# Query and key stores of a transformer block: parts in tiles of their own, the subtraction on VectorE for half of the work, reads spread over steps

## The chip, the core and the metric

The kernel runs on one core of one Trainium2 chip. The metric is the device time in microseconds (us). The kernel before took 2427.64 us (median of three runs, 2426.45 to 2430.05). One more run was profiled; it took 2427.2 us, and all times below that are not called a median are from it.

## The reference

The program is one conditioned transformer block on `x` of 2 x 2048 x 512 in float32. The rows of the batch are called row 0 and row 1.

```python
mod = silu(condition) @ Wada + bada
sh_a, sc_a, gt_a, sh_m, sc_m, gt_m = split(mod, 6, axis=1)
xm = layernorm(x, g1, be1) * (1 + sc_a) + sh_a
x = x + gt_a * attention(xm, Wqkv, Wproj, bproj)      # 16 heads of 32, causal
xm = layernorm(x, g2, be2) * (1 + sc_m) + sh_m
h = gelu(xm @ W1 + b1)                                # 512 -> 2048
x = x + gt_m * (h @ W2 + b2)                          # 2048 -> 512
```

The change touches the stage that makes queries, keys and values (`xm @ Wqkv`), once for each row of the batch.

## The kernel before, in words

**Order of the stages.** Queries, keys and values of row 0 (0 to 241 us of the profile), attention of row 0 (to about 780 us), projection of row 0 with the start of row 1, queries, keys and values of row 1 (841 to 1060 us), attention of row 1, its projection, and the two feed-forward layers for all tokens.

**A group and a unit.** `Qkv.run` (lines 1017 to 1075) takes the 2048 tokens of a row in four groups of 512. A group has six units: four of `keys_and_queries`, one for each 128 channels, and two of `values`. A unit multiplies 2 x 2 blocks with seven products in place of eight (Strassen's scheme in the form of Winograd), so it has seven steps, each of two products of 128 x 128 by 256. After each step `tick` counts one; a group has 42 ticks. The last step of a unit (`direct`) is made after the first two steps of the next one. The first unit of row 0 is made in a plain way instead (`plain`). From the second group on, `tick` also issues score products of the attention to come, as many as a plan of costs says.

**High and low parts.** Queries and keys are stored as a rounded part (hi, type float32r) and the rest (lo). `split` (line 940) rounds a tile of 128 x 512 with ScalarE (line 943) and subtracts that from the value with GpSimd (line 944). Both parts lie in one tile `hl` of two halves; the low half also serves as the accumulator while the unit's products come in. ScalarE writes a first partial result into it (line 938), VectorE adds others (lines 950 and 956). There are four such tiles, so two units' worth, and a tile is free when its store has landed.

**Stores and reads back.** `stored` (line 905) writes a tile to DRAM in one transfer of 512 KB. After the keys of the first unit of a group, it issues eight reads of 256 KB from DRAM right away (lines 319 and 336): they spread the first four heads' keys and queries over the partitions as attention wants them, and they need the stores just issued to have landed. All these transfers are issued by SP, whose queue works in order.

**What else uses the queues.** In the same stages weights for the feed-forward layers are prepared by `Pieces` (line 1077): SP reads a piece (lines 1102, 1111), GpSimd makes four sums of it for the seven-product scheme (line 1123), and GpSimd's own queue stores it (lines 1139, 1143). The reads and sums go by tick numbers in `pieces.plan` (lines 1384 and 1440). A piece of the first layer is read as 4 x 128 KB and stored as 896 KB; a piece of the second as 8 x 128 KB, stored as 7 x 448 KB. `load_wada` (line 1249) reads 2 MB of modulation weights in ticks 7 and 56 of row 0.

**Who sets the order.** TensorE's products and the operations wrapped in `act` keep the order of the program text; the rest is placed by the scheduler of the tile layer when the program is built. Each engine then works through its list in order, so an instruction that waits holds up all that stands behind it on its engine.

Of the kernel before, what the change touches and what calls it, by code (L numbers as in the profile page):

```python
# [8 lines left out]
F32 = mybir.dt.float32  # L9
# [18 lines left out]
def dit_block_kernel(  # L28
# [264 lines left out]
    class Row:  # L293
# [18 lines left out]
        def load_keys(self, c, g, n=1):  # L312

            for q in range(g, g + n):
                tok = slice(q * MT, (q + 1) * MT)
                t = self.key_tile(c, q)
                self.kst[c, q] = t
                for r in range(4):
                    nc.sync.dma_start(
                        t[r * HD : (r + 1) * HD].bitcast(F32),  # L320
                        kd[self.b][c][r % 2, :, tok].rearrange("(h d) t -> d h t", d=HD),
                    )
# [9 lines left out]
        def load_queries(self, u):  # L332
            c, i = units[u]
            t = bp.tile([P, HC, QB], F32R, tag="qst", name="qst", bufs=AHEAD + 1)
            for r in range(4):
                nc.sync.dma_start(
                    t[r * HD : (r + 1) * HD].bitcast(F32),
                    qd[self.b][c][r // 2, :, i * QB : (i + 1) * QB].rearrange(
                        "(h d) t -> d h t", d=HD
                    ),  # L340
                )
            self.qst[u] = t
# [440 lines left out]
    class Qkv:  # L783
# [6 lines left out]
        def __init__(self, row, qp, psum):  # L790
            self.row, self.qp, self.psum = row, qp, psum
            self.xts, self.xmT, self.ops = {}, {}, {}
            self.w = qp.tile([P, 7, HK, D], F32, tag="wqk", name="wqk")
            self.t = {
                n: qp.tile([P, HK, HALF_T], F32, tag=f"t{n}", name=f"t{n}")
                for n in (S1, S2, A22)
            }
# [107 lines left out]
        def stored(self, g, f, which, hl):  # L905
# [4 lines left out]
            nc.sync.dma_start(  # L910
                dst[:, :, tok].rearrange("l p t -> p l t"), hl.bitcast(F32)
            )
            if f == 0 and which == 1:
                row.load_keys(0, g)
                row.load_queries(g)

        def keys_and_queries(self, g, f, hp):

            ops = self.operands(g)
            hls = [  # L920
                hp.tile([P, 2, MT], F32R, tag="hl", name="hl", bufs=4) for _ in range(2)
            ]

            def part(i, j):
                d = hls[i].bitcast(F32)
                return d[:, 1, j * HALF_T : (j + 1) * HALF_T]
# [13 lines left out]
            def split(i):  # L940
                hl = hls[i]
                d = hl[:, 1].bitcast(F32)
                nc.scalar.copy(hl[:, 0], d)  # L943
                nc.gpsimd.tensor_tensor(hl[:, 1], d, hl[:, 0].bitcast(F32), ALU.subtract)  # L944
                self.stored(g, f, i, hl)
# [18 lines left out]
        def plain(self, g, f, hp):  # L964
# [3 lines left out]
            for which in range(2):  # L968
                box = []
                for k in range(C):  # L970
                    def run(which=which, k=k, box=box):
# [7 lines left out]
                        if k < C - 1:  # L979
                            return  # L980
                        hl = hp.tile([P, 2, MT], F32R, tag="hl", name="hl", bufs=4)
                        scale = HD**-0.5 if which == 0 else 1.0
                        nc.scalar.activation(hl[:, 0, :], box[0], AF.Copy, scale=scale)
                        nc.vector.scalar_tensor_tensor(
                            hl[:, 1, :], box[0], scale, hl[:, 0, :].bitcast(F32),
                            ALU.mult, ALU.subtract,
                        )
                        self.stored(g, f, which, hl)
# [28 lines left out]
        def run(self, hp, also, early=()):  # L1017
# [3 lines left out]
            for g in range(NG):  # L1021
                at = [0]

                def tick():
# [15 lines left out]
                    if g > 0 and n == 2:  # L1040
                        self.token_sum(g, A22)
                    also(g, n)
# [31 lines left out]
            for step in late:  # L1074
                step()

# [155 lines left out]
    with pool("wada") as wp, pool("qkv0") as qp, pool("hl0") as hp, pool(  # L1232
# [138 lines left out]

        def room_k():
# [12 lines left out]
        for f, (room, load, start) in enumerate((  # L1385
            (room_v, 4, 12), (room_v, 25, 36), (room_v, 46, 54), (room_k, 56, 63),
            (room_q, 66, 73), (room_k, 80, 87), (room_q, 91, 98), (room_k, 105, 112),
# [9 lines left out]
    with pool("qkv1") as qp, pool("ps_qkv1", bufs=6, space=PSUM) as ps_mm:  # L1397
# [29 lines left out]
        with pool("hl1") as hp:  # L1427
# [12 lines left out]
            for f, (room, load, start) in enumerate((  # L1440
                (room_2, 0, 6), (room_1, 16, 24), (room_2, 39, 46),
# [549 lines left out]
```

## Time and profile before

| | us |
|---|---|
| median of three runs | 2427.64 |
| profiled run: its time | 2427.2 |
| profiled run: its span, first to last instruction | 2424.7 |
| TensorE busy in the span | 2326.1 (96%) |
| VectorE, ScalarE, GpSimd busy | 1404.1, 1009.9, 1147.5 |
| granted TensorE clock, mean | 0.985 |

TensorE's busy share is 96% over the whole span, but the page's row of forty slices shows it lower in the first two slices and in the fifteenth and sixteenth, which lie in the stages of queries, keys and values. "Busy" in such a row includes time at a lowered clock, so a row of the granted clock stands beside it. The share of the DMA engines is the mean over 16 engines of the time that packets took; in these rows it can go slightly over 1.

### The profile page before, as it was taken

The page shows a single profiled execution, that of the slowest core. Times are in us where ns is not written, and L with a number is a line of the kernel's source. Part 1 is how long each engine was busy: PE and PEld are TensorE (multiplying, and loading weights), DVE is VectorE, ACT ScalarE, POOL GpSimd, SP SyncE. Part 2 cuts the span into 40 slices and gives each one's busy share as a digit, 9 for nine tenths or more (in the row PEclk, how much of TensorE's full clock was granted, in tenths as well). Part 3 has the DMA queues.
Part 4 walks back from the last instruction along what each step waited for, and adds up shares of the span by engine and source line. Part 5 has one row for each costly group of instructions (what it writes and reads, how often), then busy time and mean ns, then how long its engine had stood idle before and what let it go on. Part 6 is the DMA issues. An engine that isn't in the chain of part 4 may idle for free.

```text
span 2424.7 us, 34152 instructions
## 1 busy us (share of the span) xinstructions
PE 2326.1 (96%) x12033; PEld 1413.6 (58%) x12033; DVE 1404.1 (58%) x2930; ACT 1009.9 (42%) x1952; POOL 1147.5 (47%) x1291
## 2 busy tenths in 40 slices
PE   5799999999999977999999999999999999999998
PEld 3687555555554466865555555444486487477467
DVE  3366766666665623676677667474274365366356
ACT  3343555555556133345555555532332332332321
POOL 7441798878884594239889787651000000000000
PEclk9899999999999988999999999999999999999999
DMA  8865323241132775461412313254253353444333
GB/s 288 298 201 164 72 58 79 62 97 40 49 135 79 256 262 175 135 165 40 102 40 75 74 32 113 93 181 165 76 174 131 121 169 122 148 145 141 135 121 126
DMA packets 159492, 311.61 MB, mean 129 GB/s; under 512 B 15520, under 2 KB 47820, under 8 KB 157528
## 3 DMA queue, kind: packets, MB, share of 16 engines
q1 hardware_dynamic: 154464, 285.52, 38.7%
q0 software_dynamic: 4480, 23.36, 2.4%
q8 instruction: 94, 1.54, 0.3%
q14 instruction: 78, 0.64, 0.1%
q10 hardware_dynamic: 376, 0.55, 0.1%
HBM read 229.95 MB, written 87.29 MB: 131 GB/s over the span
## 4 chain that ended last, share of the span: by engine, by line
PE 82%; DMA 5%; POOL 5%; issue 3%; DVE 2%; SPq 1%; ACT 1%; POOLq 0%; DVEq 0%; ACTq 0%
PE ps_a L204 20%; PE st L204 19%; PE o L204 11%; PE ps_b L204 10%; PE s L204 9%; PE ps_c L204 5%; PE sm L204 4%; PE ps_o L204 3%; DMA k<-hl 2%; DMA q<-hl 1%; POOL kst L1123 1%; POOL hl L944 1%; PE ps_xt L212 1%; POOL ee L621 1%; DVE mx L468 1%
## 5 line engine op out<-in xcount | busy, mean ns | idle before, releaser
L593 ACT ACTIVATE e<-st 128x512 f32<-128x512 f32 (+1 forms) x1152 | 573.8, 579 | 429.5 <-PE st L204 369.8
L621 POOL TENSOR_TENSOR ee<-ee,e 128x512 f32<-128x512 f32 x424 | 528.9, 1285 | 4.4 <-ACT e L593 4.2
L468 DVE TENSOR_REDUCE mx<-s 128x1 f32<-128x512 f32 x604 | 407.4, 687 | 198.7 <-PE s L204 197.5
L204 PE MATMUL s<-kst,qst 128*128 128x512 f32 (+3 forms) x1032 | 419.1, 410 | 6.8 <-DVE mx L468 6.3
L204 PE MATMUL st<-qst,kst 128*128 128x512 f32 (+3 forms) x1280 | 409.3, 387 | 0.0
L204 PE MATMUL ps_a<-sum,w 128*128 128x256 f32 (+1 forms) x1088 | 346.6, 454 | 0.0
L204 PE MATMUL o<-e,vv 128*32 128x512 f32 (+3 forms) x2560 | 300.6, 538 | 1.9 <-POOL e L599 1.9
L463 DVE CUSTOM_DVE_ANT_0 junk<-s,causal 128x512 bf16<-128x512 f32 (+3 forms) x428 | 208.7, 488 | 136.2 <-PE s L204 128.8
L204 PEld LDWEIGHTS st<-qst,kst 128*128 128x128 f32 x1280 | 227.5, 188 | 94.0 <-issue 61.9
L204 PEld LDWEIGHTS ps_a<-sum,w 128*128 128x128 f32 x1088 | 206.4, 190 | 109.7 <-issue 91.3
L204 PEld LDWEIGHTS s<-kst,qst 128*128 128x128 f32 x1032 | 195.3, 189 | 120.9 <-DVE mx L468 58.7
L621 POOL TENSOR_TENSOR ee<-e 128x512 f32<-128x512 f32 x168 | 210.5, 1286 | 103.0 <-ACT e L593 102.7
L944 POOL TENSOR_TENSOR hl<-hl 128x512 fp32r<-128x512 f32 x62 | 78.8, 1270 | 198.8 <-ACT hl L943 166.6
L599 POOL TENSOR_SCALAR_AFFINE_SELECT e<-e 128x128 f32<-128x128 f32 (+1 forms) x384 | 121.9, 350 | 99.3 <-ACT e L593 96.5
L204 PE MATMUL st<-fold,sel 32*128 32x512 f32 (+1 forms) x1152 | 148.6, 481 | 0.5
L204 PEld LDWEIGHTS st<-fold,sel 32*128 32x128 f32 x1152 | 59.2, 181 | 143.2 <-ACT e L593 86.8
L1570 DVE TENSOR_TENSOR h<-c,ps_b 128x512 f32<-128x512 f32 x32 | 22.0, 687 | 202.4 <-PE ps_b L204 202.4
L204 PEld LDWEIGHTS o<-e,vv 128*32 128x32 f32 x2560 | 61.4, 108 | 101.7 <-issue 78.8
L204 PE MATMUL ps_b<-sum,w 128*128 128x256 f32 (+1 forms) x384 | 120.6, 450 | 0.0
L1744 ACT ACTIVATE h<-h,cols 128x512 f32<-128x512 f32 x96 | 69.2, 722 | 118.6 <-DVE h L1570 118.6
L468 DVE TENSOR_REDUCE mx<-st 128x1 f32<-128x512 f32 x164 | 112.6, 687 | 4.1 <-PE st L204 1.3
L204 PE MATMUL ps_a<-t,wqk 128*128 128x256 f32 x248 | 67.2, 400 | 39.3 <-ACT hl L938 37.4
(204 smaller groups left out, 3095.4 us busy)
## 6 DMA issues: line engine op xcount, KB each, us to landing
qst<-q SPq DMA_DIRECT2D x128, 256.0 KB
kst<-k SPq DMA_DIRECT2D x128, 256.0 KB
w<-w1d SPq DMA_DIRECT2D x32, 896.0 KB
w<-w2d SPq DMA_DIRECT2D x28, 1024.0 KB
w<-w2d SPq DMA_DIRECT2D x28, 768.0 KB
q<-hl SPq DMA_DIRECT2D x32, 512.0 KB
k<-hl SPq DMA_DIRECT2D x32, 512.0 KB
o<-ot SPq DMA_DIRECT2D x32, 256.0 KB
```

Source lines behind the costliest of these rows:

```text
L204: return tc.keep_in_program_order(nc.tensor.matmul(*args, **kw))
L212: return tc.keep_in_program_order(nc.tensor.transpose(dst, src, ident[:n, :n]))
L463: nc.vector.tensor_tensor_reduce(junk[:, :w], s[:, :w], causal[:, QB - w :], 1.0, MASKED, ALU.add, ALU.max, m,)
L468: nc.vector.tensor_reduce(m, s[:, :w], axis=AX.X, op=ALU.max)
L593: act(nc.scalar.activation(e[:, :w], sts[h][:, :w], AF.Exp))
L599: nc.gpsimd.affine_select(d, d, pattern=[[0, len(tiles)], [1, P]], compare_op=ALU.is_ge, fill=0.0, base=0, channel_multiplier=-1,)
L621: act(engine.tensor_tensor(dst, x, y, ALU.add))
L944: nc.gpsimd.tensor_tensor(hl[:, 1], d, hl[:, 0].bitcast(F32), ALU.subtract)
L1123: nc.gpsimd.tensor_tensor(part(n), part(x), part(y), op)
L1570: act(nc.vector.tensor_tensor(dst, x, y, ALU.add))
L1744: nc.scalar.activation(d, ps, AF.Gelu, bias=col(r_b1 + half * HF + f, 1))
```

## The change

Six edits, all in the stage of queries, keys and values:

1. The tile `hl` of two halves becomes two tiles, `hi` and `lo`. There are three `hi` tiles, and five `lo` tiles for row 0, six for row 1.
2. `stored` issues two transfers of 256 KB, one for each part, in place of one of 512 KB.
3. The subtraction that makes the low part runs on VectorE for the first two groups of a row, and on GpSimd as before for the other two.
4. The eight reads back of keys and queries are kept in a list, and `tick` issues one of them in each tick from the tenth on.
5. In row 0 the pieces of the first feed-forward layer are read and summed later: the first is summed from tick 38 (before 12), the others are read from tick 58 on (before 25), and the last uses another part of the value tile as its room.
6. In row 1 the third piece of the second layer is read at tick 47 and summed from tick 56 (before 39 and 46).

```diff
@@ -312,14 +312,20 @@
         def load_keys(self, c, g, n=1):
 
             for q in range(g, g + n):
-                tok = slice(q * MT, (q + 1) * MT)
-                t = self.key_tile(c, q)
-                self.kst[c, q] = t
-                for r in range(4):
-                    nc.sync.dma_start(
-                        t[r * HD : (r + 1) * HD].bitcast(F32),
-                        kd[self.b][c][r % 2, :, tok].rearrange("(h d) t -> d h t", d=HD),
-                    )
+                for load in self.key_loads(c, q):
+                    load()
+
+        def key_loads(self, c, q):
+            tok = slice(q * MT, (q + 1) * MT)
+            t = self.kst[c, q] = self.key_tile(c, q)
+
+            def load(r):
+                nc.sync.dma_start(
+                    t[r * HD : (r + 1) * HD].bitcast(F32),
+                    kd[self.b][c][r % 2, :, tok].rearrange("(h d) t -> d h t", d=HD),
+                )
+
+            return [lambda r=r: load(r) for r in range(4)]
 
         def key_tile(self, c, q):
             tag = f"kst{c % 2}{q}"
@@ -330,16 +336,23 @@
             return self.key_tile(0, q).bitcast(F32).rearrange("p h t -> p (h t)")
 
         def load_queries(self, u):
+            for load in self.query_loads(u):
+                load()
+
+        def query_loads(self, u):
             c, i = units[u]
             t = bp.tile([P, HC, QB], F32R, tag="qst", name="qst", bufs=AHEAD + 1)
-            for r in range(4):
+            self.qst[u] = t
+
+            def load(r):
                 nc.sync.dma_start(
                     t[r * HD : (r + 1) * HD].bitcast(F32),
                     qd[self.b][c][r // 2, :, i * QB : (i + 1) * QB].rearrange(
                         "(h d) t -> d h t", d=HD
                     ),
                 )
-            self.qst[u] = t
+
+            return [lambda r=r: load(r) for r in range(4)]
 
         def load_sums(self, u0, u1):
 
@@ -789,7 +802,7 @@
 
         def __init__(self, row, qp, psum):
             self.row, self.qp, self.psum = row, qp, psum
-            self.xts, self.xmT, self.ops = {}, {}, {}
+            self.xts, self.xmT, self.loads = {}, {}, []
             self.w = qp.tile([P, 7, HK, D], F32, tag="wqk", name="wqk")
             self.t = {
                 n: qp.tile([P, HK, HALF_T], F32, tag=f"t{n}", name=f"t{n}")
@@ -907,23 +920,24 @@
             row, b = self.row, self.row.b
             tok = slice(g * MT, (g + 1) * MT)
             dst = (qd if which == 0 else kd)[b][f]
-            nc.sync.dma_start(
-                dst[:, :, tok].rearrange("l p t -> p l t"), hl.bitcast(F32)
-            )
+            for n in range(2):
+                nc.sync.dma_start(dst[n, :, tok], hl[n].bitcast(F32))
             if f == 0 and which == 1:
-                row.load_keys(0, g)
-                row.load_queries(g)
+                self.loads = row.key_loads(0, g) + row.query_loads(g)
+
+        def hi_tile(self, hp):
+            return hp.tile([P, MT], F32R, tag="hi", name="hi", bufs=3)
+
+        def lo_tile(self, hp):
+            return hp.tile([P, MT], F32R, tag="lo", name="lo", bufs=5 + self.row.b)
 
         def keys_and_queries(self, g, f, hp):
 
             ops = self.operands(g)
-            hls = [
-                hp.tile([P, 2, MT], F32R, tag="hl", name="hl", bufs=4) for _ in range(2)
-            ]
+            los = [self.lo_tile(hp) for _ in range(2)]
 
             def part(i, j):
-                d = hls[i].bitcast(F32)
-                return d[:, 1, j * HALF_T : (j + 1) * HALF_T]
+                return los[i].bitcast(F32)[:, j * HALF_T : (j + 1) * HALF_T]
 
             def product(ps, n, new):
                 for k in range(HK):
@@ -938,11 +952,12 @@
                 nc.scalar.activation(part(i, j), ps, AF.Copy, scale=scale)
 
             def split(i):
-                hl = hls[i]
-                d = hl[:, 1].bitcast(F32)
-                nc.scalar.copy(hl[:, 0], d)
-                nc.gpsimd.tensor_tensor(hl[:, 1], d, hl[:, 0].bitcast(F32), ALU.subtract)
-                self.stored(g, f, i, hl)
+                hi, lo = self.hi_tile(hp), los[i]
+                d = lo.bitcast(F32)
+                nc.scalar.copy(hi, d)
+                engine = nc.vector if g < 2 else nc.gpsimd
+                engine.tensor_tensor(lo, d, hi.bitcast(F32), ALU.subtract)
+                self.stored(g, f, i, (hi, lo))
 
             def last(ps, i, j):
                 d = part(i, j)
@@ -978,14 +993,13 @@
                         )
                         if k < C - 1:
                             return
-                        hl = hp.tile([P, 2, MT], F32R, tag="hl", name="hl", bufs=4)
+                        hi, lo = self.hi_tile(hp), self.lo_tile(hp)
                         scale = HD**-0.5 if which == 0 else 1.0
-                        nc.scalar.activation(hl[:, 0, :], box[0], AF.Copy, scale=scale)
+                        nc.scalar.activation(hi, box[0], AF.Copy, scale=scale)
                         nc.vector.scalar_tensor_tensor(
-                            hl[:, 1, :], box[0], scale, hl[:, 0, :].bitcast(F32),
-                            ALU.mult, ALU.subtract,
+                            lo, box[0], scale, hi.bitcast(F32), ALU.mult, ALU.subtract
                         )
-                        self.stored(g, f, which, hl)
+                        self.stored(g, f, which, (hi, lo))
                     steps.append(run)
             return steps
 
@@ -1039,6 +1053,8 @@
                         act(nc.scalar.activation(first, eps, AF.Exp))
                     if g > 0 and n == 2:
                         self.token_sum(g, A22)
+                    if n > 9 and self.loads:
+                        self.loads.pop(0)()
                     also(g, n)
                     if g > 0 and n >= 7:
 
@@ -1073,6 +1089,7 @@
                     late = steps[6:]
             for step in late:
                 step()
+            assert not self.loads
 
     class Pieces:
 
@@ -1369,6 +1386,9 @@
         def room_v():
             return [(0, blocks_of(value_rows(row, 4, 8), w1p)[:, :7])]
 
+        def room_w():
+            return [(0, blocks_of(value_rows(row, NT - MTT, NT), w1p)[:, :7])]
+
         def room_k():
             return [(0, blocks_of(spare_k[1], w1p)[:, :7])]
 
@@ -1383,8 +1403,8 @@
 
         pieces.plan(FC // 2, room_2, 5, 17)
         for f, (room, load, start) in enumerate((
-            (room_v, 4, 12), (room_v, 25, 36), (room_v, 46, 54), (room_k, 56, 63),
-            (room_q, 66, 73), (room_k, 80, 87), (room_q, 91, 98), (room_k, 105, 112),
+            (room_v, 4, 38), (room_k, 58, 68), (room_q, 62, 73), (room_k, 84, 93),
+            (room_q, 88, 98), (room_k, 108, 116), (room_q, 112, 121), (room_w, 101, 126),
         )):
             pieces.plan(f, room, load, start)
         qkv.run(hp, also, ((0, 0),))
@@ -1438,7 +1458,7 @@
                 ]
 
             for f, (room, load, start) in enumerate((
-                (room_2, 0, 6), (room_1, 16, 24), (room_2, 39, 46),
+                (room_2, 0, 6), (room_1, 16, 24), (room_2, 47, 56),
             ), FC // 2 + 1):
                 pieces.plan(f, room, load, start)
             qkv.run(hp, also)
```

## The prediction

> **What bounds the kernel now.** I read the page first, then eight windows cut where the first products of the groups of tokens start (four of row 0, four of row 1), then who waited for the stores, then the chain of waits at single places.
>
> The windows, with TensorE's (PE) busy time, its granted clock and the share of the DMA engines near the end of each line:
>
> ```profile
> core 0: us, PE busy (x) PEld busy (x) DVE busy (x) ACT busy (x) POOL busy (x), PEclk, DMA share, GB/s
> 26.48:82.58 56.10, 37.15 (x166) 30.31 (x164) 16.37 (x40) 22.48 (x47) 44.62 (x56) 0.88 0.94 313
> 82.58:141.25 58.67, 46.64 (x217) 38.71 (x216) 22.09 (x68) 20.38 (x45) 20.94 (x24) 0.85 0.72 237
> 141.25:192.63 51.38, 50.16 (x250) 41.32 (x249) 33.49 (x90) 17.54 (x40) 19.58 (x22) 1.00 0.57 187
> 192.63:241.00 48.37, 45.35 (x207) 37.12 (x206) 32.10 (x75) 14.98 (x33) 10.17 (x8) 1.00 0.64 177
> 840.79:906.99 66.20, 49.75 (x193) 40.70 (x192) 16.00 (x39) 20.84 (x47) 55.77 (x67) 0.85 0.77 255
> 906.99:966.75 59.76, 47.43 (x202) 40.43 (x200) 20.93 (x67) 20.27 (x45) 28.69 (x35) 0.83 0.56 188
> 966.75:1015.50 48.75, 47.30 (x226) 39.95 (x225) 32.45 (x85) 17.73 (x40) 10.15 (x8) 1.00 0.41 130
> 1015.50:1060.00 44.50, 42.89 (x196) 35.77 (x195) 30.62 (x69) 14.66 (x32) 10.16 (x8) 1.00 0.63 178
> ```
>
> The reader is to see two kinds of group. In the last two of each row TensorE idles 1.2 to 3.0 us; in the first two, which I call dense, 12.0 to 19.0 us, 59.8 us in sum, and its clock is lowered besides. In ten-us windows of these stretches, busy time times (1 - clock) sums to 19.7 us.
>
> What the engines waited for, from the view of the tile `hl`:
>
> ```profile
> L943 ACT CAST hl<-hl x62: 607/618/626, 34.6 to 1048.4; 128x512 fp32r<-128x512 f32 x62
> L944 POOL TENSOR_TENSOR hl<-hl x62: 1255/1270/1291, 38.0 to 1049.1; 128x512 fp32r<-128x512 f32 x62
> ...
>   DMA q<-hl: 27.2, 8
>   DMA k<-hl: 24.5, 9
> ```
>
> ScalarE could not start on a tile for 51.7 us because its last store had not landed; TensorE's gaps follow from that. The chain of waits shows how long a landing takes, alone and behind other transfers:
>
> ```profile
> 32.72 4.43 DMA k<-hl
> ...
> 931.89 11.90 DMA k<-hl
> ```
>
> And SP's timeline shows why the largest gap (15.27 us to 59.35) came about: eight reads back and eight 256 KB reads of modulation weights stand ahead of stores whose data had been ready for long.
>
> ```profile
> 38.95 1.38 SPq L336 DMA_DIRECT2D qst<-q  x3
> 40.38 10.30 SPq L1263 DMA_DIRECT2D vv<-in_L_cond_Wada_dram  x8
> 52.17 0.38 SPq L910 DMA_DIRECT2D q<-hl  x1
> ```
>
> The product order of TensorE is the same in the two programs as built, so the change can act only through such waits.
>
> **The tiles.** A step is two products, 0.87 us undisturbed (ps_b starts at 31.18, ps_c at 32.05). Before, a unit's key tile was that of the unit two back, free seven steps after its rounding: 7 x 0.87 = 6.1 us. In them must fit 0.62 (rounding) + 1.27 (subtraction) + 0.36 (issue, SP's rows of line 910) + 4.43 (landing) = 6.7 us. It does not fit even with no queue. After, with two thirds of a unit more, a `hi` tile is written again ten steps on, 8.7 us, for 0.62 + 0.36 + 4.43 = 5.4 us, and a key `lo` tile ten steps on for 6.1 us. So 2.6 to 3.3 us of queueing are free, where 0.6 was missing.
>
> **Reads and weight pieces.** A spread read comes a tick apart (about 1 us), so a store finds few of them ahead, not 2 MB. In row 0's first group the modulation weights are now issued before the reads back, when the queue holds 1.5 MB of pieces at most; the first stores then follow at about 39 us, not 52. Of row 0's pieces, three reads (0.5 MB each) and two stores (0.9 MB each) leave the dense groups: 3.4 MB, at 313 GB/s / 0.94 = 333 GB/s 10.2 us of all DMA engines. They go to groups three and four, whose share rises from 0.57 and 0.64 by 10.2 us in 99.8; hidden there behind TensorE, price 1 us, up to 7 if a burst meets the reads back. Row 1's third piece moves 8 to 10 ticks and stays in the same group: nothing, or 3 us either way.
>
> **What is late next is the DMA.** Shares times lengths: 52.7 + 42.2 + 51.0 + 33.5 = 179.4 us of work in the dense groups, 169.2 without the moved pieces, in 240.7 us. TensorE's floor there is 240.7 - 59.8 - 19.7 + 3.2 (two gaps of 1.9 and 1.3 us of another cause) = 164. So the DMA engines need as long as TensorE. How full can they be? The first group reaches 0.94; the first 100 us of the kernel 0.85. I take 0.90: 169.2 / 0.90 = 188, a gain of 53 us; at 0.94 61, at 0.85 42. With the floor alone it would be 76.
>
> **The subtraction on VectorE.** 30 subtractions leave GpSimd (30 x 1.27 = 38 us), whose dense groups in row 1 are full: 55.77 of 66.20 busy. VectorE gets 30 x 0.69 (line 877, same shape) = 21 us in some 190, at 40% load: room enough. But it is a wait in VectorE's in-order list: behind it stand the additions of lines 950 and 956 and the score maxima. A product into the bank read by 956 comes two steps later, so 1.74 us of delay are free. And the two engines get in each other's way:
>
> ```profile
> L877 DVE TENSOR_TENSOR t<-xmT,t x16: 650/692/6049, 22.4 to 1015.7; 128x512 f32<-128x512 f32 x16
> ...
> 820.20 1.25 POOL L1210 TENSOR_TENSOR xt<-xt,bgate 128x512 f32<-128x512 f32 x1
> ...
> 819.63 6.05 DVE L877 TENSOR_TENSOR t<-xmT,t 128x512 f32<-128x512 f32 x1
> ```
>
> Of 14 such VectorE operations beside GpSimd's work, 13 took 0.67 to 2.03 us and one 6.05, until GpSimd paused. A 6.05 costs TensorE 6.05 - 0.69 - 1.74 = 3.6 us; the others nothing. About 19 of the 30 will meet GpSimd at work (6 in the first group, 2 in the second, 8 and 3 in row 1). I take two long ones among the eight of row 1's first group, where GpSimd is unbroken, and one in fourteen of the other 11: 2.8 x 3.6 = 10, less 2 for GpSimd's relief in row 1's third gap, 8 us. Bounds: 0, and all 19 long, 69 us.
>
> The Trainium skill (SBUF — State Buffer, "SBUF: two separate sides") says that a VectorE operation with two SBUF inputs and a reading GpSimd operation exclude each other for a whole instruction, whoever starts first. By that a wait would end with one GpSimd operation, 1.27 us, inside the free 1.74, and the price would be 0, the sum 8 us lower; the row of 6.05 us says that it can be several.
>
> **Two stores for one.** 64 more issues x 0.36 = 23 us of SP, which waited 73.2 us for line 944 in row 0's stage alone. In full stretches some of it delays a store: 2 us; 0 to 6. [...] In the trace eight 256 KB reads were taken in 10.30 us, 1.3 us each against 4.43 for a landing alone, so they overlap.
>
> **Sum.** 53 - 8 - 2 - 1 = 42 us. 2427.2 - 42 = 2385; the median is 0.4 us above the profiled run, which does not matter here. About 0.2% (5 us) is what a measurement of this kernel can tell from no change.
>
> **Rivals.**
>
> *The DMA engines give back half.* For it: shares of 1.02 to 1.04 in 40 to 80 us and 100 to 120 us, where even stores issued first landed after 8 to 12 us, more than the 8.7 us a tile now has. Against it: those followed 2 MB bursts. If such landings stay, each of four units in four dense groups still loses 1 to 2 us, and row 0's gaps only shrink: gain 10 to 28, about 2407.
>
> *VectorE starves behind GpSimd: slower.* One mechanism, in row 1's first group and row 0's first, where GpSimd sums pieces without a pause. It decides from the point where a contended subtraction takes 0.69 + 1.74 + 50/19 = 5.1 us in the mean; at 6.05 for all 19 it costs 69 against 50 gained: about 2446. For it: the 6.05 row, with the same kind of GpSimd work. Against: 13 of 14.
>
> *It does not do what it says.* Three `hi` tiles are fewer than four `hl` tiles; if rounding waits for them as long as the first write did, the 51.7 us stand under another name, time within 5 us of before. Against: ten steps for 5.4 us.
>
> **How the numbers follow.** Forecast (gain 29 to 70) 0.61; DMA half 0.19; starved, slower 0.15; nothing 0.05. Faster 0.80, same 0.05, slower 0.15. The range runs from 2358 (0.94 full, no price for VectorE, and some of the 7.3 us of idle time in the light groups) to 2424, which leaves out the starved case and a part of the even one. The forecast's own range is 2358 to 2398.
>
> **What the profile after would show.** Right: the four dense groups at 43, 50, 52 and 52 us or less, no gap of TensorE over 5 us there, clock back near 1, ScalarE's waits for stores below 20 us, DMA share near 0.9 in the dense groups. VectorE's subtraction would read 0.7 us with a tail. Wrong: a subtraction row with a mean above 2 us and gaps released by VectorE (starved), or gaps before rounding released by the `hi` stores (DMA). A gain or loss outside the two stages would refute the whole account.

## The result, and the profile after

The changed kernel takes 2358.3 us (median; 2357.26 to 2361.37) where the kernel before took 2427.05 on the same chip: a ratio of 0.9716, 95% interval 0.9700 to 0.9733. That is 69 us faster, where the forecast was 42. The measured time is 0.3 us inside the range of the forecast (2358 to 2424). In a second measurement the changed kernel took 2357.27 us, 0.7 us outside that range and 71.0 us faster than before (0.9705, 0.9682 to 0.9728). So it is luck that the first one lies inside. The profiled execution took 2359.31 us, with a span of 2357.5 and a mean granted clock of 0.997 (before: 0.985).

The windows view of the kernel after, one row for each group of tokens (four of row 0, four of row 1), cut at the same instructions of TensorE as the rows shown of before to within 2 us; PEclk is the granted clock, the figure after it the share of the DMA engines:

```profile
core 0: us, PE busy (x) PEld busy (x) DVE busy (x) ACT busy (x) POOL busy (x), PEclk, DMA share, GB/s
26.11:68.58 42.47, 37.84 (x169) 31.46 (x168) 18.09 (x35) 18.63 (x40) 34.54 (x45) 0.96 0.94 320
68.58:112.98 44.40, 43.04 (x217) 36.11 (x216) 26.52 (x76) 20.06 (x45) 6.62 (x8) 1.00 0.83 247
112.98:170.23 57.25, 52.84 (x250) 42.23 (x249) 39.57 (x101) 20.86 (x47) 26.60 (x30) 0.97 0.82 261
170.23:216.19 45.96, 45.27 (x208) 37.56 (x207) 32.12 (x76) 15.12 (x34) 14.15 (x14) 1.00 0.61 191
815.65:857.21 41.56, 40.87 (x194) 34.86 (x193) 24.23 (x33) 17.60 (x42) 34.64 (x39) 1.00 0.87 280
857.21:899.47 42.26, 41.00 (x202) 35.88 (x201) 26.59 (x75) 19.51 (x44) 34.61 (x47) 1.00 0.96 325
899.47:950.80 51.33, 49.10 (x226) 41.13 (x225) 35.82 (x96) 21.23 (x46) 10.15 (x8) 0.97 0.55 176
950.80:994.50 43.70, 43.01 (x197) 36.02 (x196) 31.74 (x74) 14.43 (x32) 10.18 (x8) 1.00 0.51 150
```

The reader is to see three things. The dense groups (first two of each row) lost most of their idle time, which fell from 59.8 to 7.9 us, and their lowered clock, of which only row 0's first group keeps some (0.96). The third group of row 0 is longer than before, 57.25 us against 51.38, with a DMA share of 0.82 against 0.57. The fourth groups are a little shorter. The table below has the same lengths for both kernels, cut at exactly the same TensorE instructions:

| group | row 0: 1 | 2 | 3 | 4 | row 1: 1 | 2 | 3 | 4 |
|---|---|---|---|---|---|---|---|---|
| before, us | 57.8 | 58.7 | 51.4 | 48.8 | 66.2 | 59.8 | 48.8 | 45.6 |
| after, us | 42.5 | 44.4 | 57.3 | 46.0 | 41.6 | 42.3 | 51.3 | 43.7 |
| after, second measurement, us | 41.4 | 46.3 | 56.5 | 46.0 | 40.7 | 43.3 | 49.7 | 43.7 |

The dense groups fell from 242.4 to 170.7 us, 71.7 in all; the third groups gave back 8.4 of it and the fourth groups added 4.7. The two executions of the same kernel differ by up to 1.9 us in a group, so smaller differences are not read below; and one execution further down differs by 6 us in a group that its edit does not touch, so a length of one execution is a hint and the medians decide. Outside the two stages nothing moved by more than 2 us.

The view of the tile `lo`, which shows its writers (min/median/max ns) and, with DMA, what ScalarE, VectorE and GpSimd together waited for (us, times):

```profile
L957 ACT CAST hi<-lo x62: 603/618/626, 34.2 to 989.5; 128x512 fp32r<-128x512 f32 x62
L959 POOL TENSOR_TENSOR lo<-lo,hi x32: 1259/1272/1283, 118.5 to 990.2; 128x512 fp32r<-128x512 f32 x32
...
L959 DVE TENSOR_TENSOR lo<-lo,hi x30: 673/732/4144, 34.9 to 902.6; 128x512 fp32r<-128x512 f32 x30
...
  DMA q<-lo: 14.5, 3
  DMA k<-hi: 2.9, 1
```

Of these 17.4 us, 13.4 are GpSimd's, ahead of subtractions in row 1's third and fourth groups, where it idles most of the time, and 1.1 are VectorE's. ScalarE, whose 51.7 us of before these waits are to be compared with, waited 2.9 us here for `k<-hi` and another 1.9 us for `q<-hi`, 4.8 in all. VectorE's subtraction costs 0.73 us in the median. SP's timeline has the first stores at 40.00 us, ahead of most of the reads back, where they stood at 52.17 ("first" leaves out the unit that is made in the plain way):

```profile
33.81 5.21 SPq L1280 DMA_DIRECT2D vv<-in_L_cond_Wada_dram  x8
39.26 0.33 SPq L323 DMA_DIRECT2D kst<-k  x1
40.00 0.34 SPq L924 DMA_DIRECT2D q<-hi  x1
40.64 0.32 SPq L924 DMA_DIRECT2D q<-lo  x1
41.27 3.43 SPq L323 DMA_DIRECT2D kst<-k  x3
```

The longest gap left to TensorE in the two stages is 3.49 us, up to 48.68. The chain of waits puts it down to the landing of one of those first stores, behind the modulation weights:

```profile
35.04 5.54 DMA vv<-in_L_cond_Wada_dram
...
40.64 7.49 DMA q<-lo
...
48.15 0.39 ACT lo L952
```

### The profile page after: what moved, and what is told of

Read it like the earlier page. It is cut to its first block, busy times and chain, and to the rows that moved or that the text cites. A ratio compares the mean times of both kernels' runs of the same rounds, so it can differ in the third digit from the quotient of the medians.

```text
span 2357.5 us, 34284 instructions
## 1 busy us (share of the span) xinstructions
PE 2311.3 (98%) x12033; PEld 1403.5 (60%) x12033; DVE 1433.9 (61%) x2960; ACT 1008.0 (43%) x1952; POOL 1120.0 (48%) x1261
## 4 chain that ended last, share of the span: by engine, by line
PE 92%; DVE 3%; DMA 2%; POOL 1%; ACT 1%; issue 1%; SPq 0%; DVEq 0%; POOLq 0%; ACTq 0%
PE ps_a L204 24%; PE st L204 20%; PE ps_b L204 12%; PE o L204 11%; PE s L204 10%; PE ps_c L204 6%; PE sm L204 4%; PE ps_o L204 3%; PE ps_xt L212 1%; POOL ee L634 1%; DVE mx L481 1%; PE ps_o L212 1%; DVE junk L476 0%; DMA x<-in_x_dram 0%; DMA q<-lo 0%
## 5 line engine op out<-in xcount | busy, mean ns | idle before, releaser
L959 POOL TENSOR_TENSOR lo<-lo,hi 128x512 fp32r<-128x512 f32 x32 | 40.7, 1273 | 134.2 <-ACT hi L957 113.9
L204 PEld LDWEIGHTS ps_b<-sum,w 128*128 128x128 f32 x384 | 73.0, 190 | 37.2 <-issue 30.6
```

The lines of the kernel that those rows point to most:

```text
L204: return tc.keep_in_program_order(nc.tensor.matmul(*args, **kw))
L959: engine.tensor_tensor(lo, d, hi.bitcast(F32), ALU.subtract)
```

## The experiments

Two theories explain the gaps of before. A, the prediction's: a tile was needed again sooner than its store could land (6.1 us against 6.7 by the prediction's sum, which is taken up under "VectorE alone"), so the number of tiles is the main cause. B: the tiles would have done, and what made stores late was the order in the queues, GpSimd's subtraction behind piece sums in row 1 and SP's stores behind reads in row 0.

A gain is the median of before, measured beside it, less the kernel's median. The changed kernel's own two gains, 68.8 and 71.0, have the mean 69.9; a loss is 69.9 less a kernel's gain, uncertain by about 5 us if one goes by the intervals in the table. The lengths are those of each kernel's profiled execution, cut as in the table above.

| kernel | gain, us | ratio, 95% interval | row 0: 1 | 2 | 3 | 4 | row 1: 1 | 2 | 3 | 4 |
|---|---|---|---|---|---|---|---|---|---|---|
| after, subtraction on GpSimd | 49.5 | 0.9791 (0.9774 to 0.9807) | 43.4 | 45.3 | 63.3 | 46.0 | 47.4 | 47.0 | 51.9 | 43.7 |
| after, reads at once | 48.8 | 0.9800 (0.9785 to 0.9814) | 59.9 | 44.1 | 53.7 | 47.4 | 41.5 | 44.8 | 51.0 | 43.8 |
| after, tiles for two units | 35.6 | 0.9851 (0.9836 to 0.9866) | 49.9 | 58.5 | 53.2 | 49.8 | 47.5 | 50.3 | 51.0 | 45.9 |
| after, pieces as before | 58.4 | 0.9758 (0.9744 to 0.9773) | 41.7 | 46.6 | 56.5 | 46.9 | 41.5 | 50.8 | 48.9 | 43.7 |
| before, tiles and stores alone | 40.1 | 0.9835 (0.9813 to 0.9857) | 56.5 | 47.7 | 51.5 | 47.4 | 40.7 | 58.5 | 50.9 | 43.7 |
| before, order alone | 24.3 | 0.9897 (0.9879 to 0.9915) | 48.7 | 54.3 | 53.2 | 49.8 | 63.7 | 49.7 | 49.5 | 45.9 |
| before, VectorE alone | 2.8 | 0.9985 (0.9975 to 0.9996) | 63.5 | 56.5 | 52.1 | 50.6 | 67.0 | 50.4 | 49.1 | 45.7 |
| after, row 1's third piece as before | 62.9 | 0.9739 (0.9726 to 0.9752) | 43.0 | 44.2 | 56.6 | 46.0 | 41.4 | 50.6 | 48.9 | 43.7 |
| after, two piece reads later | 70.4 | 0.9716 (0.9694 to 0.9738) | 41.5 | 44.7 | 54.2 | 46.0 | 47.5 | 44.8 | 51.3 | 43.7 |
| after, VectorE in all groups | 59.2 | 0.9762 (0.9747 to 0.9776) | 43.5 | 46.4 | 56.9 | 46.7 | 41.6 | 42.3 | 55.1 | 43.9 |
| after, a third store | 58.7 | 0.9760 (0.9747 to 0.9774) | 44.1 | 43.7 | 58.0 | 46.0 | 41.5 | 48.0 | 54.2 | 43.7 |

### One part undone at a time

**Tiles for two units.**

```diff
-            return hp.tile([P, MT], F32R, tag="hi", name="hi", bufs=3)
+            return hp.tile([P, MT], F32R, tag="hi", name="hi", bufs=4)
-            return hp.tile([P, MT], F32R, tag="lo", name="lo", bufs=5 + self.row.b)
+            return hp.tile([P, MT], F32R, tag="lo", name="lo", bufs=4)
```

> The kernel after with four hi and four lo tiles, two units' worth as the four hl tiles of before (the part of edit 1 that adds tiles undone); stores are still one for each part. Theory A: the key's lo tile is again needed seven steps after its rounding, 6.1 us for some 6.1 to 6.7 us of work (subtraction 0.69 in place of 1.27 in the first two groups), every unit waits whenever anything queues: loss 25 to 45 us (2383 to 2403), over all four dense groups. Theory B: loss below 10 us.

Loss 34 us, as A had it, in all four dense groups and, 2 to 4 us each, in the fourth ones. The tiles are still two for each unit's part here, so the loss is that of their number. The view of the tile `lo` shows the wait back under its old name, the key's store (these lines are the waits, us and times; of the first, six with 27.0 us are ScalarE's):

```profile
  DMA k<-lo: 29.3, 7
  DMA k<-hi: 7.2, 3
  DMA q<-lo: 5.3, 5
```

**Subtraction on GpSimd.**

```diff
-                engine = nc.vector if g < 2 else nc.gpsimd
+                engine = nc.gpsimd
```

> The kernel after with the subtraction of all four groups back on GpSimd (edit 3 undone), all else kept. Theory A (the tile that is needed again before its store has landed is the main cause; with ten steps for 6.1 us it no longer is): the slack of 2.6 to 3.3 us takes up most of GpSimd's queue, so it loses less than 10 us against the kernel after (2358 to 2368). Theory B (what made the stores late was the queue ahead of them: piece sums on GpSimd in row 1, reads on SP in row 0; the number of tiles matters little): the subtraction again stands behind piece sums, loss 25 to 40 us (2383 to 2398), nearly all in the first two groups of row 1, with gaps of TensorE released by rounding after a store.

Loss 20 us, between the two: A's 10 is clearly passed, B's 25 missed by about the uncertainty, and half of it lies in row 1's dense groups (5.8 and 4.7 us). The waits of SP there, in a window of 810 to 1010 us (us in total, times, longest):

```profile
SPq L924 <- POOL lo L959: 59.3, 27, 9.1
```

In the kernel after the same window has

```profile
SPq L924 <- ACT hi L957: 73.8, 17, 14.8
SPq L924 <- POOL lo L959: 12.2, 15, 1.0
```

So SP stood for up to 9.1 us at a store whose lo tile GpSimd had not delivered, with everything behind it in its list. The largest gap of row 1's dense groups, 3.61 us up to 851.88, comes even without SP: GpSimd subtracts at 849.68, behind sums of weights, from a tile that was rounded at 835.80, and ScalarE's next rounding waits for that hi tile.

```profile
848.33 1.35 POOL kst L1140 x2
849.68 1.22 POOL lo L959
...
850.92 0.62 ACT hi L957
...
851.88 1.22 PE ps_a L204 x2
```

In row 0's third group, which has GpSimd's subtraction in both kernels, 6 us more were lost while VectorE waited for `x`. The order of the queues shows why `x` was late: a subtraction of the second group stood ahead of a piece's last sum on GpSimd, so that piece was stored at 117.29 (110.86 in the kernel after); SP waited 3.5 us for this store to land before it read the next piece into the same room, and came to the rest of `x` at 125.46 (120.12).

**Reads at once.**

```diff
-                self.loads = row.key_loads(0, g) + row.query_loads(g)
+                row.load_keys(0, g)
+                row.load_queries(g)
```

> The kernel after with the reads of keys and queries issued at once, eight behind the key's store, as before (edit 4 undone). Theory A: the tiles' slack hides it, loss up to 10 us. Theory B: stores again wait behind 2 MB of reads, loss 10 to 20 us, mostly in the first two groups of row 0, where the weight pieces share the DMA engines, and 2 to 6 us in row 1.

Loss 21 us, what B expected for row 0 and more than A allowed. It is mainly one place: row 0's first group, 17.4 us longer, with a gap of 12.73 us up to 56.05. Row 1 lost 2.5 us at most.

**Pieces as before.**

```diff
-            (room_v, 4, 38), (room_k, 58, 68), (room_q, 62, 73), (room_k, 84, 93),
-            (room_q, 88, 98), (room_k, 108, 116), (room_q, 112, 121), (room_w, 101, 126),
+            (room_v, 4, 12), (room_v, 25, 36), (room_v, 46, 54), (room_k, 56, 63),
+            (room_q, 66, 73), (room_k, 80, 87), (room_q, 91, 98), (room_k, 105, 112),
...
-                (room_2, 0, 6), (room_1, 16, 24), (room_2, 47, 56),
+                (room_2, 0, 6), (room_1, 16, 24), (room_2, 39, 46),
```

> The kernel after with the weight pieces of both rows read and summed when they were before (edits 5 and 6 undone). By the prediction's step (3.4 MB leave row 0's dense groups, 10.2 us of DMA work, and the first stores come at 39 us rather than 52): loss 10 to 20 us in the first two groups of row 0, a few us won back in row 0's third group, where the moved reads delayed an x tile in the kernel after (5.9 us slower than before there); row 1 within 3 us. If the DMA engines are no bound in the dense groups, the loss is below 5 us in sum.

Loss 11.5 us, but not where it was expected. Row 0's dense groups lost 1.4 us together, below what can be read, and its third group stayed long (56.5): no gain or loss there is shown to come from the pieces' new times. Row 1's second group lost 8.5 us.

**Row 1's third piece alone.** It is read from step 39 and summed from step 46, where the kernel after reads it from 47 and sums it from 56. With 42 ticks a group that moves the reads from the end of the first group to the start of the second.

```diff
-                (room_2, 0, 6), (room_1, 16, 24), (room_2, 47, 56),
+                (room_2, 0, 6), (room_1, 16, 24), (room_2, 39, 46),
```

> The kernel after with only row 1's third weight piece summed from step 39, as before, and not from step 47. The prediction's step: nothing, or 3 us either way. What the kernel with all pieces as before showed (8.5 us lost in row 1's second group, with VectorE's subtraction at 3.27 us beside GpSimd's sums, 2.4 us won back in the third): loss of 5 to 10 us, so that this one move, not row 0's pieces, makes most of the 11 us.

Loss 7 us, 8.3 in the second group against 2.4 won in the third. The expectation looked for VectorE's subtraction; the trace shows SP instead. Its timeline has the piece's eight reads ahead of `x` and of the next unit's stores:

```profile
857.33 1.91 SPq L1128 DMA_DIRECT2D kst<-in_L_cond_W_dram  x2
...
862.41 1.84 SPq L816 DMA_DIRECT2D x<-in_x_dram  x4
864.35 1.32 SPq L924 DMA_DIRECT2D q<-hi  x1
```

and the chain of waits there goes through that store, whose tile the next rounding waits for:

```profile
864.35 8.70 DMA q<-hi
...
873.14 0.63 ACT hi L957
```

A gap of 5.49 us up to 877.53 follows. In the kernel after, the store stands ahead of the reads and lands in less time, in the same view:

```profile
862.71 5.01 DMA q<-hi
```

### One part alone

**Tiles and stores alone**: the kernel after with the subtraction, the reads and the pieces as before.

```diff
-                engine = nc.vector if g < 2 else nc.gpsimd
+                engine = nc.gpsimd
-                self.loads = row.key_loads(0, g) + row.query_loads(g)
+                row.load_keys(0, g)
+                row.load_queries(g)
...
-            (room_v, 4, 38), (room_k, 58, 68), (room_q, 62, 73), (room_k, 84, 93),
-            (room_q, 88, 98), (room_k, 108, 116), (room_q, 112, 121), (room_w, 101, 126),
+            (room_v, 4, 12), (room_v, 25, 36), (room_v, 46, 54), (room_k, 56, 63),
+            (room_q, 66, 73), (room_k, 80, 87), (room_q, 91, 98), (room_k, 105, 112),
...
-                (room_2, 0, 6), (room_1, 16, 24), (room_2, 47, 56),
+                (room_2, 0, 6), (room_1, 16, 24), (room_2, 39, 46),
```

> The kernel before with edits 1 and 2 alone: hi and lo in tiles of their own for three units, a store for each; subtraction on GpSimd, reads at once, pieces as before. Put back one at a time, the kernel after lost 20 us (GpSimd subtraction), 21 us (reads at once), 34 us (two units of tiles) and 11 us (pieces), 87 in sum for a change that is worth 69, so the parts cover for each other. Theory A (slack of the tiles is the main cause): gain against the kernel before of 25 to 45 us. Theory B (order in the queues): gain below 15 us, and the first large gap at 59 us stands, since the stores still wait behind 2 MB of reads and 2 MB of weights.

Gain 40.1 us: A's range, and the largest part. Row 0's second group and row 1's first are nearly where the full change has them (47.7 and 40.7). But both of B's places are still there. In row 0's first group a gap of 14.97 us stands up to 57.55; SP's timeline:

```profile
40.09 8.38 SPq L1281 DMA_DIRECT2D vv<-in_L_cond_Wada_dram  x8
48.86 0.33 SPq L924 DMA_DIRECT2D q<-hi  x1
```

In row 1's second group a gap of 9.27 us ends at 888.85. The chain of waits leads through GpSimd's list, SP's list and the read of `x` to VectorE's list, where an addition stood behind the statistics of `x`:

```profile
873.43 2.02 POOL vv L1141 x3
...
876.03 0.73 POOL vv L1141
876.76 1.24 POOL lo L960
...
878.02 0.32 SPq L924
...
882.52 5.24 DMA x<-in_x_dram
...
888.39 0.41 DVE lo L972
...
888.85 1.22 PE ps_a L204 x2
```

The first two lines are piece sums, the third the subtraction of a key tile that was queued behind them; SP stores it at 878.02, and only then comes to `x`.

**Order alone**: a store for each part, spread reads, later pieces; tiles for two units, subtraction on GpSimd.

The diff is against the kernel after:

```diff
-            return hp.tile([P, MT], F32R, tag="hi", name="hi", bufs=3)
+            return hp.tile([P, MT], F32R, tag="hi", name="hi", bufs=4)
-            return hp.tile([P, MT], F32R, tag="lo", name="lo", bufs=5 + self.row.b)
+            return hp.tile([P, MT], F32R, tag="lo", name="lo", bufs=4)
-                engine = nc.vector if g < 2 else nc.gpsimd
+                engine = nc.gpsimd
```

> The kernel before with a store for each part, spread reads and the later pieces (edits 2, 4, 5, 6), but tiles for two units and the subtraction on GpSimd. Theory A: the landing path of 6.7 us does not fit into 6.1 us, so the gain is below 25 us, and each unit of the dense groups still waits for the store of its lo tile. Theory B: gain of 25 to 40 us.

Gain 24.3 us, just inside what A allowed and just short of what B asked; the interval, 20.6 to 29.4 us, reaches into both, so the time decides nothing. The first gap of 15 us is gone (48.7 for the first group), while row 1's first group keeps 63.7 of its 66.2 us. There the chain of waits stays on GpSimd's list of sums and subtractions from 853 to 872 us, which this kernel leaves as it was. So B's whole order without the added tiles is not this kernel but the one with tiles for two units above: gain 35.6 us.

**VectorE alone**: the kernel before with one line changed.

```diff
-                nc.gpsimd.tensor_tensor(hl[:, 1], d, hl[:, 0].bitcast(F32), ALU.subtract)
+                engine = nc.vector if g < 2 else nc.gpsimd
+                engine.tensor_tensor(hl[:, 1], d, hl[:, 0].bitcast(F32), ALU.subtract)
```

> The kernel before with the subtraction of the first two groups on VectorE (edit 3 alone), still one hl tile and one store for both parts. The path from rounding to free tile becomes 6.1 us for 6.1. Theory A: gain of 0 to 12 us, a few in row 1. Theory B: gain of 20 to 35 us, nearly all in row 1, whose stores waited behind piece sums on GpSimd.

Gain 2.8 us (0.9985, 0.9975 to 0.9996): the range that A gave, but not by A's reason. A's sum of 6.7 us adds 0.36 us of issue to a landing of 4.43 us, while a landing in these views counts from the start of that issue (SP's row and the landing both start at 32.72). Without the issue the path is 6.3 us in the kernel before and 5.7 here. And that store stood right behind ten reads of pieces (1.3 MB, issued from 27.07 to 32.62 us); other stores of the kernel before landed in less, with which the path is 5.5 us there:

```profile
976.05 3.65 DMA k<-hl
...
1024.64 3.58 DMA k<-hl
```

So it is not shown that a store was too late for 6.1 us with nothing in its way. With the subtraction on VectorE the path had 0.4 us to spare by A's own row, and ScalarE still waited 50.8 us for stores. What the tiles were short of is time for stores that queue. Row 1's second group won 9.4 us, and row 0's first lost 5.7.

**The kernel after itself, on the chip of these three.**

> The kernel after itself, to have its time on the chip of these runs: 2356 to 2362 us, 65 to 72 us below the kernel before. Every theory expects the same.

2357.27 us, gain 71.0. The parts undone one at a time add to 87 us, more than the whole. Some of them therefore need each other, and do not cover for each other, as the expectation for the tiles alone had it. It is clearest for GpSimd's subtraction: to be rid of it is worth 2.8 us while tiles and reads hold the groups up anyway, and 20 once they don't. The tiles do not depend on the rest in that way: they are worth 40 us alone and 34 on top of the rest, and the rest is worth 36 us without them and 31 on top of them (the split stores count in both when alone).

Neither theory holds alone. The tiles are the largest single part (A), and the two places that B named, the reads ahead of row 0's first stores and GpSimd's list, are each worth some 20 us that the slack of the tiles does not take up. Together the parts of B are worth about as much as the tiles.

### What bounds it now

**Two of row 0's piece reads later**, behind `x`.

```diff
-            (room_v, 4, 38), (room_k, 58, 68), (room_q, 62, 73), (room_k, 84, 93),
-            (room_q, 88, 98), (room_k, 108, 116), (room_q, 112, 121), (room_w, 101, 126),
+            (room_v, 4, 38), (room_k, 58, 68), (room_q, 62, 73), (room_k, 90, 98),
+            (room_q, 94, 103), (room_k, 108, 116), (room_q, 112, 121), (room_w, 101, 126),
```

> The kernel after with two of row 0's piece reads six steps later, behind the x tile of the third group's end on SP. If the piece read of 3.9 us ahead of x is what costs row 0's third group its 5.9 us: 3 to 6 us faster than the kernel after (2352 to 2355), with VectorE's wait for x gone. If the DMA engines, above 0.9 busy there, set the pace: no difference, within 2 us.

Median 2356.18 us, gain 70.4: not told from the kernel after. In place, the third group of row 0 fell to 54.2 us (56.5 and 57.3 after), its clock went back to 1.00 from 0.97, and VectorE's wait for `x` stayed at 2.19 us. That fits a part of that group's loss, 2 to 3 us, coming from the reads ahead of `x`, but does not show it: the wait that was to go stayed, and this execution, the slowest of its four (2367.41 us), lost 6 us in row 1's first group, where the edit changes nothing.

**A third store**: more DMA work of the same kind, in the dense groups alone.

```diff
+    qs, ks = [
+        [[dram.tile([P, T], F32, tag=f"{t}{b}{c}", name=f"{t}{b}{c}") for c in range(C)]
+         for b in range(B)]
+        for t in ("sq", "sk")
+    ]
...
             for n in range(2):
                 nc.sync.dma_start(dst[n, :, tok], hl[n].bitcast(F32))
+            if g < 2:
+                again = (qs if which == 0 else ks)[b][f]
+                nc.sync.dma_start(again[:, tok], hl[0].bitcast(F32))
```

> The kernel after with a third store for each key and query tile of the first two groups of each row: the hi part once more, into a place of its own that nothing reads. 32 transfers of 256 KB, 8.4 MB; at 333 GB/s that is 25 us of all DMA engines, put into 171 us of dense groups whose DMA engines already worked 154 us. If those engines set the pace of the dense groups, as the prediction's main term had it (0.90 full): 25 / 0.9 = 28 us slower, 20 at the least. If DMA work that a group has no time for only runs on into the next group, beside TensorE: below 10 us, with the third groups' DMA share up by 10 us or more of work.

Loss 11.2 us, far from the 20 and, within the uncertainty, near the 10. Share times length over the eight groups rose by 22.6 us, from 279.0 to 301.6; 14 us of it stayed in the dense groups, which became 6.6 us longer, and 9 us ran on into the third groups, which became 3.6 longer. The windows of row 1's second and third group, which lost most:

```profile
857.49:905.49 48.00, 42.88 (x201) 37.20 (x200) 27.13 (x74) 19.04 (x43) 32.70 (x45) 0.96 0.92 307
905.49:959.70 54.21, 49.61 (x227) 41.60 (x225) 36.65 (x97) 21.48 (x48) 10.10 (x8) 0.94 0.60 197
```

So a microsecond of DMA work costs half a microsecond here, or a quarter to three quarters by the uncertainty of the loss, and that is a bound from above. The edit also adds 32 issues on SP, and the third store holds its hi tile until it has landed: ScalarE waited 5.1 us for these stores. The DMA engines are not what sets the pace of the dense groups; what their work costs by itself is not told apart.

**VectorE in all groups.**

```diff
-                engine = nc.vector if g < 2 else nc.gpsimd
+                engine = nc.vector
```

> The kernel after with the subtraction on VectorE in all four groups. If VectorE pays only for long operations beside GpSimd: it is busy 31 to 36 of 44 to 57 us in the last two groups, 32 more at 0.7 us fit in, and the time stays within 3 us. If VectorE's list is the next bound there: 5 to 15 us slower, with gaps released by maxima of scores.

Loss 10.7 us, in the range named for VectorE's list as the bound. The largest piece, beside which the rest of the loss is left unexplained, is row 1's third group, 3.8 us, with a gap of 3.95 us up to 921.79. It is not released by maxima but by ScalarE's normalization of `x`, which waited for statistics that VectorE reached late; VectorE's timeline lists no idle time from 909 to 920 us but 0.17, and the statistics stand behind a subtraction:

```profile
916.58 0.69 DVE L959 TENSOR_TENSOR lo<-lo,hi 128x512 fp32r<-128x512 f32 x1
...
917.66 0.69 DVE L216 BATCH_NORM_STATS2 stat<-x 128x6 f32<-128x512 f32 x1
...
918.68 1.25 DVE L216 BATCH_NORM_STATS2 stat<-x 128x6 f32<-128x512 f32 x2
```

Leaving the subtraction of the last two groups on GpSimd, which is idle most of the time there (10.15 of 51.33 us busy in row 1's third group), is right.

## Why the prediction was right, and where not

**The tiles** were right as the place, and as the largest single cause: worth 40 us alone with the split stores, 34 when undone, with the key's store named again as what ScalarE waits for. The sum behind them was not: it counted SP's issue twice and took a store behind 1.3 MB of reads for one alone, so "It does not fit even with no queue" is not shown (5.5 to 6.3 us for 6.1). One part was too small: the fourth groups gained 2 to 3 us each by the slack, where the sum had nothing for the light groups.

**"What is late next is the DMA"** is the step that failed. It made the gain in the dense groups 53 us, 43 after the prices of VectorE and of the stores, where 71.7 came. The step took all DMA work of these groups as work that has to be done inside them, 169.2 us. Shares times lengths after are 39.9 + 36.9 + 36.2 + 40.6 = 153.6 us: 15.6 were not done there. They ran on. The third groups' work rose from 49.3 to 75.2 us, by 25.9, of which the prediction had at most the 10.2 us of moved pieces. In bytes (rate times length of the rows) the dense groups moved 59.6 MB before and 49.9 after, the third groups 16.0 and 24.0; row 1's third group, into which no piece was moved, went from 6.3 to 9.0. A read back or a piece has no fixed date in a group, and only the transfers that a tile or `x` waits for do. The run with a third store shows the same on its own: 22.6 us of added work cost 11, not all of it by the work. That the fill came out at the foretold 0.90 (153.6 in 170.7) is chance: TensorE was busy 162.8 of these 170.7 us, so it, and not the DMA, set their length.

**The price of what runs on** was put at 1 us; the third groups lost 8.4. Row 0's third group is short where the two groups before it were long and long where they were short: 51.4, 51.5, 52.1, 53.2, 53.2 and 53.7 us after about 103 us or more, 54.2 to 63.3 after 86 to 90. It fits work that is pushed on, since the pieces' old times left it at 56.5; but that it is the DMA work was argued and not shown.

**The subtraction on VectorE** was priced at 8 us for long rows beside GpSimd. No run has this price by itself; the rows make it near 0 in the dense groups. In nine runs with VectorE's subtraction in the dense groups alone, 10 of 270 such rows took more than the free 0.69 + 1.74 = 2.43 us, the longest 4.15; the estimate had 2.8 in 30. The 4.14 in the kernel after, beside GpSimd's sums, was followed by no gap (its timeline, VectorE's line first):

```profile
838.74 4.14 DVE L959 TENSOR_TENSOR lo<-lo,hi 128x512 fp32r<-128x512 f32 x1 [2.29 <-ACT hi L957]
```

```profile
839.01 1.28 POOL L846 TENSOR_TENSOR wv<-wv 128x512 f32<-128x512 f32 x1
840.23 2.09 POOL L1140 TENSOR_TENSOR kst<-kst 128x256 f32<-128x256 f32 x3
```

The Trainium skill's rule (SBUF — State Buffer, "SBUF: two separate sides"), which made this price 0, was by these rows nearer in the sum than the one long row that the prediction set against it. (The price of 0 makes the gain 8 us higher and the time 8 us lower.) As a description the rule does not cover this row: by it a wait should end with one GpSimd operation, and four ran beside the subtraction here. And the credit of 2 us for GpSimd's relief was far too small: with the other parts in, moving the subtraction is worth 20.

**Reads and pieces.** The first stores were foreseen at 39 us and came at 40.00. That is worth 17 us in that group (reads at once again). The 3.4 MB that leave row 0's dense groups are worth nothing that can be read there. **Row 1's third piece**, "nothing, or 3 us either way", is worth 7: the step looked at which group the sums fall in, took the reads to stay in it too, and did not look at what stands behind eight reads on SP.

**Two stores for one** (2 us) were in every kernel with the new tiles and were not measured by themselves.

**The rivals.** DMA engines that give back half: a landing of 7 to 9 us does occur (7.49 at 40.64), and it makes the longest gap left. But the dense groups idle 7.9 us in all, where this rival had 16 to 32 (1 to 2 us in each of 16 units). Its shares "of 1.02 to 1.04 in 40 to 80 us" hold to 70 us; the window from 70 to 80 has 0.94. VectorE starved behind GpSimd: no, by the 10 in 270. A change that does not do what it says: no, ScalarE's waits for stores fell to 4.8 us.

**What the profile was to show**: dense groups of 43, 50, 52 and 52 us or less (42.5, 44.4, 41.6, 42.3), no gap over 5 us (3.49), ScalarE's waits for stores below 20 (4.8), a DMA share near 0.9 (0.90 in the mean), a subtraction of 0.7 us with a tail. All of it came so, but the lengths were forecast 6 to 10 us too long in three of the four groups.

**The range.** Its lower end had the DMA 0.94 full (61 us), no price for VectorE and some of the 7.3 us of idle time in the light groups. That adds to 68 us at most, with nothing taken off for the stores and the pieces, and the end was put at 69. The measured 69 is another sum: 71.7 in the dense groups and 4.7 in the fourth ones, less 8.4 in the third ones. It meets the end of the range by chance.

## What to carry to other kernels

Compare how long a tile lasts before it is written again with the landing time of what must leave it, and take the landing times of all such stores in the trace, not one of them: here 5.5 to 6.3 us of path for 6.1 us of tile left no room for a store that had to queue, and room for it was worth 34 to 40 us. When such a stall goes, count the transfers that have a waiter and those that only have to be done some time; a bound from all DMA work of a stretch was too strict here, since the second kind ran on into the next stretch. What it costs there was not settled. On an in-order queue the place of a burst of reads can matter more than its volume: eight reads moved eight steps, from ahead of `x` and of a store to behind them, were worth 7 us. And try a part both alone and last: one that was worth 3 us alone was worth 20 here once the others were in.

## What the runs showed that was not expected

- A store of 256 KB took 8.70 us to land with eight piece reads and an `x` tile issued in the 7 us before it, and 5.01 us with the `x` tile ahead and the piece reads behind it. The share of the DMA engines over the whole group was lower in the slow case (0.83 against 0.96).
- VectorE's subtraction is worth very different amounts alone and last, 2.8 and 20 us. The tiles are not (40 and 34, alike within the uncertainty).
- VectorE's subtraction ran 3 to 4 us in single cases at other places in each execution, with the same program (4.14 at 838.7 us in one, 3.08 at 107.3 in another), so one profile does not tell where such a row will stand.
